# A dedicated pool for the loop's first-layer buffers, and a second level of Strassen's rule for one more product of the first MLP layer

## The chip, the cores and the metric

The kernel runs on one core of a Trainium2 chip, in one launch. The core has five engines with instruction streams of their own: PE (TensorE, matrix products; PEld is its loading of weights), DVE (VectorE), ACT (ScalarE), POOL (GpSimd) and SP (SyncE, which here only issues DMAs). [...] The metric is the device time of one execution in microseconds (us), median of several runs.

## The reference

Layer 0 is a deformable attention block with an MLP behind it, layer 1 a full self-attention block, on x of 2 x 512 x 32 x 32, all in float32. The change touches the end of the position-bias loop and the MLP of layer 0:

```python
bias = jnp.sign(pos) * jnp.log1p(jnp.abs(pos))
bias = jax.nn.relu(bias @ cpb_w1 + cpb_b1)          # 2 -> 128
bias = jax.nn.relu(bias @ cpb_w2 + cpb_b2)          # 128 -> 128
bias = (bias @ cpb_w3 + cpb_b3).reshape(b, GROUPS, H * W, Hd * Wd)
...
out = jnp.einsum('bchw,oc->bohw', out, out_w) + out_b[None, :, None, None]
x = x + out
xn2 = _bn(x, bn2_g, bn2_b)
h1 = jax.nn.gelu(jnp.einsum('bchw,oc->bohw', xn2, mlp_w1) + mlp_b1[None, :, None, None], approximate=False)
return x + jnp.einsum('bchw,oc->bohw', h1, mlp_w2) + mlp_b2[None, :, None, None]
```

`mlp_w1` is 2048 x 512 and `mlp_w2` is 512 x 2048. Layer 1 follows, and is not touched.

## The kernel before

**Order of the work.** From about 38 to 1881 us a loop of 256 steps runs the bias MLP: `st_layer1` builds h1 (128 x 4096) on DVE, `st_layer2` multiplies it on PE, ACT and DVE evict, and DMAs that add fold the results (`u`, `uo`, `uc`, `ub`). After that come the output projection (`project`), the MLP of layer 0 in eight units, and the attention of layer 1. Instructions are traced by a framework that allocates tiles in pools, inserts the semaphores, and settles at compile time the order on each engine; `tc.issue_after` pins one instruction behind another on its engine.

**Pools.** All buffers of the loop lie in one pool, `lp`: three h1 buffers of 16 KB a partition, and those named rx, u8, uo, uc, u4, ub, fb, ta, tb. When `lp` has been closed, the pools `xq` (`xs`, the residual x of 32 KB a partition, and `tx`) and `wp` (weights) are opened over the same addresses. The sixteen loads of `xs` (L1012, queue SP) are the first to use them; `project` reads `xs`.

**The eight units.** A unit is (b, p): image b, and quarter p of the 2048 hidden channels. Units 0 to 3 are image 0, units 4 to 7 image 1. Each has two halves:

- `layer1`: hidden = w1 quarter (512 x 512) times xb (512 x 1024). One level of the Strassen-Winograd rule turns it into seven products of 256 x 256 by 256 x 512. `PARTS[q]` names the sums of weights and of data that product q needs. Six of the seven (1 and 6, 4 and 7, 5 and 3, three sets) are split a second time by `twice`: seven steps, each one matmul per product of 128 x 128 by 128 x 256. The seventh, product 2, is plain: four matmuls of 128 x 128 by 128 x 512 (`second`, at time 21 among the steps; in unit 0 `first` at the start and `merge` at 21). In the trace every matmul stands as two instructions.
- `layer2`: w2 quarter times hidden, seven products of 256 x 256 by 256 x 512 by `multiply`, in the order 2, 1, 3, 5, 6, 7, 4.

`twice` puts the steps of the three sets in one order on PE by their times: set g has its products 1, 2, 6, 5, 7, 4, 3 at 7g + 0, 1, 3, 4, 6, 9, 12; fills such as the plain product have times of their own. So the tail of a unit on PE is: step 3 of set 1 (19), step 7 of set 2 (20), the plain product (21), step 4 of set 2 (23), step 3 of set 2 (26), and then layer 2. A step's sum grows in one PSUM bank: step 6 adds onto what ACT has just copied out of step 1, step 7 onto step 6, step 4 onto step 7, each after ACT's copy (L166, L170, L172, L176). DVE adds the rest (`plus`, L137): in `done(1)` c22, then c21, and ACT's `gelu(2)` (two instructions at L1096) makes the operand `hm[:, 2]` of layer 2's first product.

**PSUM.** Four tiles of two banks each are handed out in turn (`Turns`).

**Second-level sums.** `xe` holds the sums for the data (once for an image, on DVE: `sums`, `part`), `w1e` those for the weights: `load_inner` copies three blocks by SP DMAs (L996) and adds onto them by a chain of POOL DMAs (`gather`, L979). There is one `w1e` buffer, so the next unit's copies start when the last step has read it. Both leave out position 0, the operand of the plain product. Behind that chain POOL issues the adds for the unit after (w1x, w1t), and then folds w2t with four adds of its own (L119).

**Around images.** In unit 3 `normalise(1)` and the sums for image 1 are made, in unit 4 `finish(0)`, in unit 6 `blocks(0)` for layer 1, all beside the products.

Of the kernel before, what the change touches and what calls it, by code (L numbers as in the profile page):

```python
# [8 lines left out]
F32 = mybir.dt.float32  # L9
AF = mybir.ActivationFunctionType  # L10
ALU = mybir.AluOpType
# [3 lines left out]
P = 128  # L15
# [42 lines left out]
def conv_seq_kernel(ctx: ExitStack, tc: tile.TileContext, x, xt, kst, pst, cst, vec, wsm, outw, w1, w2, wl, wlt, brow, out):  # L58
# [62 lines left out]
    def spread(x, which=range(4)):  # L121
        for i in which:
            if i % 2 == 0:
                o, u = ((4, 0), (1, 3))[i // 2]
                nc.vector.tensor_tensor(x[o], x[u], x[1], ALU.subtract)  # L125
# [10 lines left out]
    def plus(out, a, b_, op=ALU.add):  # L136
        nc.vector.tensor_tensor(out, a, b_, op)  # L137
# [43 lines left out]
    FIRST_W, FIRST_X = (1, 0, 2, 3, 4, 5, 6), (1, 4, 0, 6, 5, 2, 3)  # L181
    AT_W, AT_X = ((0, 0), (1, 0), (1, 1), (0, 1)), ((0, 0), (0, 1), (1, 0), (1, 1))

    def inner_w(w, we, at=slice(1, 7), e=slice(0, 6)):
        return [w[:, at, k, P * n : P * n + P] for k, n in AT_W] + [we[:, e, j, :] for j in range(3)]

    def inner_x(x, xe, at=slice(1, 7), e=slice(0, 6)):
        return [x[:, at, k, 256 * n : 256 * n + 256] for k, n in AT_X] + [xe[:, e, j, :] for j in range(3)]


    def op_blocks(b, parts, wsum):
# [12 lines left out]
    groups = [(b, k, f) for b in range(B) for k in range(NCH) for f in range(2)]  # L204
    php = tc.tile_pool(name="ph", bufs=1, side="right")
    ph = php.__enter__()
    with tc.tile_pool(name="lp", bufs=2) as lp:


        def wake(src, *sizes):  # L210
# [10 lines left out]
        nc.scalar.activation(ones, ones, AF.Identity)  # L221

        for n in range(2):
            idle = lp.tile([P, 4 * HW], F32, tag="h1", name="idle", bufs=3)
# [352 lines left out]

        wls = [lp.tile([P, 2, NCH, C], F32, tag="h1", name="wl_s", bufs=3) for _ in range(2)]  # L580
# [8 lines left out]
        gs = lp.tile([P, 2, NCH, C], F32, tag="h1", name="gs", bufs=3)  # L589

        def weights(i):
            ps = [flat("psg") for _ in range(2)]
# [77 lines left out]
        def st_layer1(s):  # L670
            ta, tb = tabs[4 * s // KT]
            j = 4 * s % KT
            h1 = lp.tile([P, H, 4, W], F32, name="h1", bufs=3)
            a = ta[:, j : j + 4, :].rearrange("p t x -> p (t x)")
            b = tb[:, j // 4].rearrange("p y t -> p (y t)")
            step = H // 2 if s == 0 else H
            for y in range(0, H, step):
                nc.vector._custom_dve(  # L678
                    TENSOR_ADD_SAT,
                    out=h1[:, y : y + step].rearrange("p y t x -> p (y t x)"),  # L680
                    in0=a.unsqueeze(1).to_broadcast([P, step, 4 * W]),
                    in1=b[:, 4 * y : 4 * (y + step)].unsqueeze(2).to_broadcast([P, 4 * step, W]),
                    s0=FMAX, s1=0.0,
                )
            h1s[s] = h1
# [286 lines left out]
    with ExitStack() as top, tc.tile_pool(name="wp", bufs=1) as wp:  # L972
# [17 lines left out]
        def load_inner(i):  # L990
            if i >= len(units):
                return
            we = wp.tile([P, 6, 3, P], F32, name="w1e")
            w = inner_w(wts[units[i]][0], we)
            for o, u in ((4, 3), (5, 0), (6, 1)):
                nc.sync.dma_start(out=w[o], in_=w[u])  # L996
            copied.append(newest(mybir.EngineType.SP))
            gather(w)
            wts[units[i]].append(we)
# [81 lines left out]
            return go  # L1081

        def sums(xb):
            xe = mp.tile([P, 6, 3, 256], F32, tag="xe", name="xe")

            def part(g):
                spread([xb[:, j] for j in FIRST_X], ((0, 1, 3), (2,), ())[g])
                spread(inner_x(xb, xe, slice(2 * g + 1, 2 * g + 3), slice(2 * g, 2 * g + 2)))

            part(0)  # L1090
            return xe, part

        def layer1(p, we, w, xb, xe, hm, others=(), early=False):
            def gelu(blk, src, scale=1.0):
                for m in range(2):
                    nc.scalar.activation(  # L1096
                        hm[:, blk, m, :], src[:, m, :], AF.Gelu,
                        bias=col("mb1", 4 * p + 2 * (blk // 2) + m), scale=scale,
                    )

            c11, c12, c21, c22, r5, r3 = (hm[:, j] for j in range(6))

            def weights(q, j):
                a = FIRST_W[PARTS[q][0]]
                return [inner_w(w, we, a, a - 1)[j]]

            def moving(q, j):
                b_ = FIRST_X[PARTS[q][1]]
                return [inner_x(xb, xe, b_, b_ - 1)[j]]

            def dest(g, m, h):
                return hm[:, 2 * g : 2 * g + 2, m, 256 * h : 256 * h + 256]

            def done(g):
                if g == 0:
                    plus(c12, c12, c11)
                elif g == 1:
                    plus(c22, c22, c12)
                    plus(c21, c21, c22)
                    gelu(2, c21, -1.0)  # L1120
                else:
                    plus(c22, c22, r5)
                    gelu(3, c22, -1.0)
                    plus(c12, c12, r5)
                    plus(c12, c12, r3)
                    gelu(1, c12)

            def second():
                ps = mq.tile([P, 2, 512], F32, tag="ps2", name="sw")
                product(w, xb)(ps, 0, 0)  # L1130
                plus(c11, c11, ps)
                gelu(0, c11)

            def first():
                ps = mq.tile([P, 2, 512], F32, tag="ps2", name="sw")
                product(w, xb)(ps, 0, 0)
                nc.scalar.copy(hm[:, 6], ps)

            def merge():
                plus(c11, c11, hm[:, 6])  # L1140
                gelu(0, c11)

            plain = ((-1, first), (21, merge)) if early else ((21, second),)
            twice(mq, ((1, 6), (4, 7), (5, 3)), weights, moving, dest, done, (*plain, *others))
            spread([hm[:, j] for j in range(7)])

        def layer2(b, p, w, hm):
# [51 lines left out]
        for i, (b, p) in enumerate(units):  # L1199

            j, k = divmod(i, NCH)
            if k == 0:
                br = cp.tile([P, C], F32, tag="kz", name="br")
                nc.sync.dma_start(out=br, in_=brow[j].partition_broadcast(P))
            wr = f_pool.tile([P, C], F32, tag="ss", name="wr")
            nc.sync.dma_start(out=wr, in_=wlt[:, i])
            with tc.issue_after(copied[-1]) if i else nullcontext():
                load_first(i + 1)
            wa, we, wb = wts.pop((b, p))
            hm = cp.tile([P, 7, 2, 512], F32, tag="big", name="hm")  # L1210
# [388 lines left out]
```

## Time and profile before

| what | us |
|---|---|
| three runs | 2612.25, 2611.08, 2612.11; median 2612.11 |
| the profiled execution: time, and its span | 2612.84, 2610.9 |
| PE busy (share of span) | 2597.0 (99%) |
| DVE, ACT, POOL busy | 2299.8 (88%), 1754.3 (67%), 1002.0 (38%) |
| granted PE clock | 0.999 |
| matmul of 128 x 512 in `layer2` and the plain product (L1077): 448 and 64 instructions | 194.0 and 28.8 busy |
| units 1, 2, 5, 7, start to next start | 45.85, 45.85, 45.90, 45.90 |
| units 3, 4, 6 | 46.35, 46.20, 46.60 |

Busy PE time counts overlapping ends, so a matmul's listed mean (0.592 us for 512 columns) is longer than the distance between two of them (0.429 us). The distances are what adds up. The 1.9 us between span and time lie outside the first and last instruction.

### The profile page before, as it was taken

To read this page: it belongs to the slowest core of one execution; us is meant where nothing else is said; L and a number is where in the kernel's file an instruction comes from. 1 tells how busy PE (TensorE), PEld (TensorE's weight loads), DVE (VectorE), ACT (ScalarE), POOL (GpSimd) and SP (SyncE) were. 2 spreads that over 40 slices of the span, in tenths; PEclk is the share of its full clock that TensorE was granted. 3 is DMA by queue.
4 is the path that set the end of the run, shared out by engine and by line. 5 is a ranking of instruction groups with operands and counts; after the bars stand their busy time and mean duration, and the time that the engine had idled before them with its cause. 6 is when DMAs were issued, how large, how long until landed. Compare 5 with 4: busy or idle time off the path is not lost.

```text
span 2610.9 us, 49091 instructions
## 1 busy us (share of the span) xinstructions
PE 2597.0 (99%) x19644; PEld 1010.0 (39%) x19644; DVE 2299.8 (88%) x1459; ACT 1754.3 (67%) x2362; POOL 1002.0 (38%) x1154
## 2 busy tenths in 40 slices
PE   9999999999999999999999999999999999999999
PEld 3332333333233233323333333333355655646656
DVE  6999999999999999999999999999776586666656
ACT  5887888888888888888788777777633242314041
POOL 1344444444444444444454445444432333200100
PEclk9999999999999999999999999999999999999999
DMA  5889999899998999899999899999787768400202
GB/s 187 173 191 194 198 195 196 193 189 191 199 190 190 187 203 203 175 192 203 190 197 189 183 193 201 191 191 194 160 201 169 149 149 170 87 16 1 73 0 57
DMA packets 179172, 431.43 MB, mean 165 GB/s; under 512 B 30817, under 2 KB 79089, under 8 KB 176257
## 3 DMA queue, kind: packets, MB, share of 16 engines
q0 software_dynamic: 108416, 275.19, 59.0%
q1 hardware_dynamic: 70096, 152.80, 17.8%
q8 instruction: 155, 2.54, 0.4%
q14 instruction: 73, 0.59, 0.1%
q10 hardware_dynamic: 432, 0.31, 0.0%
HBM read 82.16 MB, written 6.55 MB: 34 GB/s over the span
## 4 chain that ended last, share of the span: by engine, by line
PE 76%; issue 7%; DVE 6%; DMA 6%; POOL 3%; ACT 1%; DVEq 0%; SPq 0%; POOLq 0%; ACTq 0%
PE ps L695 48%; PE sw L1077 7%; PE sw L1248 7%; PE sw L160 7%; DMA u<-uc 3%; POOL u L734 2%; PE sw L1346 2%; PE sw L1024 2%; DVE h L678 1%; DVE ub L715 1%; PE psg L597 1%; DMA uc<-uc 1%; DMA u<-u 1%; DVE hm L137 1%; PE sim L825 1%
## 5 line engine op out<-in xcount | busy, mean ns | idle before, releaser
L695 PE MATMUL ps<-h,cw 128*32 128x512 f32 x16384 | 1772.6, 593 | 2.8 <-ACT rx L705 1.4
L678 DVE CUSTOM_DVE_ANT_1 h<-ta,tb 128x4096 f32<-128x4096 f32 (+1 forms) x257 | 1130.8, 4400 | 27.1 <-PE ps L695 23.1
L695 PEld LDWEIGHTS ps<-h,cw 128*32 128x32 f32 x16384 | 528.1, 110 | 1216.0 <-issue 1156.5
L705 ACT ACTIVATE rx<-ps,sc 128x1024 f32<-128x1024 f32 x512 | 567.8, 1109 | 134.9 <-PE ps L695 113.4
L734 POOL DMA_DIRECT2D u<-u x429 | 434.6, 1498 | 3.6 <-issue 2.6
L707 ACT ACTIVATE ub<-ps,sc 128x1024 f32<-128x1024 f32 x256 | 308.0, 1203 | 91.5 <-PE ps L695 90.7
L715 DVE SCALAR_TENSOR_TENSOR ub<-rx,sc,ub 128x1024 f32<-128x1024 f32 x256 | 326.7, 1276 | 5.6 <-ACT ub L707 5.6
L717 POOL DMA_DIRECT2D uo<-ub x127 | 112.1, 882 | 566.2 <-DVE ub L715 543.3
L1077 PE MATMUL sw<-hm,w2t 128*128 128x512 f32 x448 | 194.0, 592 | 0.2 <-DVE hm L125 0.2
L707 ACT ACTIVATE uo<-ps,sc 128x1024 f32<-128x1024 f32 x128 | 154.0, 1203 | 43.8 <-PE ps L695 41.4
L715 DVE SCALAR_TENSOR_TENSOR uo<-rx,sc,uo 128x1024 f32<-128x1024 f32 x128 | 163.4, 1277 | 6.0 <-ACT uo L707 5.5
L734 POOL DMA_DIRECT2D u<-uc x126 | 126.0, 1282 | 21.6 <-DMA u<-uc 20.6
L717 POOL DMA_DIRECT2D u<-ub x64 | 55.8, 872 | 182.0 <-DVE ub L715 181.8
L1077 PEld LDWEIGHTS sw<-hm,w2t 128*128 128x128 f32 x448 | 85.1, 190 | 103.9 <-issue 97.9
L717 POOL DMA_DIRECT2D uc<-ub x64 | 55.0, 860 | 182.6 <-DVE ub L715 146.1
L137 DVE TENSOR_TENSOR hm<-hm,sw 128x512 f32<-128x512 f32 x79 | 57.7, 732 | 73.5 <-PE sw L160 51.5
L1412 POOL DMA_DIRECT2D xs<-rs x6 | 7.2, 1200 | 258.7 <-DVE rs L137 258.7
L734 POOL DMA_DIRECT2D uc<-uc x63 | 105.2, 1671 | 3.1 <-DMA uc<-ub 3.1
L734 POOL DMA_DIRECT2D uc<-uo x63 | 97.9, 1554 | 19.7 <-DMA uc<-uo 19.3
L707 ACT ACTIVATE uc<-ps,sc 128x1024 f32<-128x1024 f32 x64 | 76.9, 1202 | 25.3 <-PE ps L695 21.5
L658 ACT ACTIVATE ta<-fb,vs 128x512 f32<-128x512 f32 (+1 forms) x65 | 89.1, 1374 | 6.3 <-DMA fb<-fdr 6.3
L707 ACT ACTIVATE u<-ps,sc 128x1024 f32<-128x1024 f32 x64 | 77.0, 1203 | 24.2 <-PE ps L695 21.0
(297 smaller groups left out, 2635.1 us busy)
## 6 DMA issues: line engine op xcount, KB each, us to landing
uo<-ub POOLq DMA_DIRECT2D x127, 512.0 KB, 5.5
fb<-fdr SPq DMA_DIRECT2D x64, 512.0 KB, 6.1
u<-ub POOLq DMA_DIRECT2D x64, 512.0 KB, 6.6
uc<-ub POOLq DMA_DIRECT2D x64, 512.0 KB, 6.1
u<-u POOLq DMA_DIRECT2D x63, 256.0 KB, 7.0
u<-uo SPq DMA_DIRECT2D x63, 256.0 KB, 5.8
u<-uo POOLq DMA_DIRECT2D x63, 256.0 KB, 7.5
uc<-uc POOLq DMA_DIRECT2D x63, 256.0 KB, 8.4
```

Source lines behind the costliest of these rows:

```text
L137: nc.vector.tensor_tensor(out, a, b_, op)
L160: nc.tensor.matmul(bank[:, e, :], w, x, start=(q in (1, 2, 5) and e == k == 0), stop=True, skip_group_check=True,)
L658: nc.scalar.activation(ta.rearrange("p j x -> p x j")[:, :, j0:j1], fb[:, 0, :, j0:j1], AF.Identity, bias=col("cb1"), scale=col("w1x"),)
L678: nc.vector._custom_dve(TENSOR_ADD_SAT, out=h1[:, y : y + step].rearrange("p y t x -> p (y t x)"), in0=a.unsqueeze(1).to_broadcast([P, ste ...
L695: nc.tensor.matmul(ps[32 * q : 32 * q + 32, h, :], cw2[:, 32 * z : 32 * z + 32], h1[:, 16 * h : 16 * h + 16, q, :], start=True, stop=True,)
L705: nc.scalar.activation(o, ps, AF.Relu, bias=sc[:, 4 + z : 5 + z])
L707: nc.scalar.activation(o, ps, AF.Relu, bias=sc[:, 4 + z : 5 + z], scale=sc[:, z : z + 1])
L715: nc.vector.scalar_tensor_tensor(r[1], r[0], sc[:, z : z + 1], r[1], ALU.mult, ALU.add)
L717: nc.gpsimd.dma_start(out=sums[s][1], in_=sums[s][3], accum_op=ALU.add)
L734: nc.gpsimd.dma_start(out=out, in_=in_, accum_op=ALU.add)
L1077: nc.tensor.matmul(ps[:, m, :], w[:, a, k, m * P : (m + 1) * P], x[:, b_, k, :], start=(k == 0), stop=(k == 1),)
L1248: nc.tensor.matmul(ps[:, m, :], w[:, a, k, c + m * P : c + (m + 1) * P], x[b_][:, k, :], start=(k == 0), stop=(k == nk - 1),)
```

## The change

Three things.

1. The h1 buffers, and the tiles that share them (`idle`, `wl_s`, `gs`), move from `lp` to a pool `hp` of their own, opened before `lp`.
2. In the units with p > 0 (six of eight) product 2 is split by a second level too. Its seven steps, one matmul of 128 x 128 by 128 x 256 each, are fills at the times 19.5, 20.2, 20.4, 20.6, 24 and 27 (two). `gelu(2)` moves to the fill at 24, ahead of step 7. The additions that end c11 (`merge`) and c12 (`ends`) come at 27, behind step 3 of set 2. Layer 2 of these units takes its products in the order 2, 3, 1.
3. `xe` and `w1e` get position 0 (seven entries instead of six). `xe`'s is made by `part(3)` behind layer 2 of p = 0; `w1e`'s by the same DMAs, one sixth larger, except for p = 0.

```diff
-    def inner_w(w, we, at=slice(1, 7), e=slice(0, 6)):
+    def inner_w(w, we, at=slice(0, 7)):
...
-    with tc.tile_pool(name="lp", bufs=2) as lp:
+    with tc.tile_pool(name="hp", bufs=3) as hp, tc.tile_pool(name="lp", bufs=2) as lp:
...
-            h1 = lp.tile([P, H, 4, W], F32, name="h1", bufs=3)
+            h1 = hp.tile([P, H, 4, W], F32, name="h1")
...
-            we = wp.tile([P, 6, 3, P], F32, name="w1e")
-            w = inner_w(wts[units[i]][0], we)
+            we = wp.tile([P, 7, 3, P], F32, name="w1e")
+            w = inner_w(wts[units[i]][0], we, slice(i % NU == 0, 7))
...
-            xe = mp.tile([P, 6, 3, 256], F32, tag="xe", name="xe")
+            xe = mp.tile([P, 7, 3, 256], F32, tag="xe", name="xe")
             def part(g):
-                spread([xb[:, j] for j in FIRST_X], ((0, 1, 3), (2,), ())[g])
-                spread(inner_x(xb, xe, slice(2 * g + 1, 2 * g + 3), slice(2 * g, 2 * g + 2)))
+                spread([xb[:, j] for j in FIRST_X], ((0, 1, 3), (2,), (), ())[g])
+                spread(inner_x(xb, xe, slice(2 * g + 1, 2 * g + 3) if g < 3 else slice(0, 1)))
...
+        INNER = ((19.5, 1), (20.2, 2), (20.4, 6), (20.6, 5))
...
                 elif g == 1:
                     plus(c22, c22, c12)
                     plus(c21, c21, c22)
-                    gelu(2, c21, -1.0)
+                    if not split:
+                        gelu(2, c21, -1.0)
                 else:
                     plus(c22, c22, r5)
                     gelu(3, c22, -1.0)
-                    plus(c12, c12, r5)
-                    plus(c12, c12, r3)
-                    gelu(1, c12)
+                    if not split:
+                        ends()
+
+            def ends():
+                plus(c12, c12, r5)
+                plus(c12, c12, r3)
+                gelu(1, c12)
...
+            bank = {}
+            def inner(q):
+                a, x = PARTS[q]
+                if q in (1, 2):
+                    bank[q] = mq.tile([P, 2, 512], F32, tag="ps2", name="sw")
+                ps = bank[2][:, int(q in (3, 5)), 0:256] if q in (2, 3, 5) else bank[1][:, 0, 0:256]
+                nc.tensor.matmul(
+                    ps, inner_w(w, we, 0)[a], inner_x(xb, xe, 0)[x], start=q in (1, 2, 5), stop=True,
+                    skip_group_check=True,
+                )
+                m, h = {1: (0, 0), 6: (0, 1), 7: (1, 1), 4: (1, 0)}.get(q, (1, 1))
+                n = slice(256 * h, 256 * h + 256)
+                if q in (1, 6, 7, 4):
+                    nc.scalar.activation(hm[:, 6, m, n], ps, AF.Copy, scale=1.0 if m == 0 else -1.0)
+                elif q == 5:
+                    plus(c11[:, m, n], c11[:, m, n], ps, ALU.subtract)
+            def seventh():
+                gelu(2, c21, -1.0)
+                inner(7)
+            def close():
+                inner(3)
+                inner(4)
+                top = c11[:, 0, :].rearrange("p (h n) -> p h n", h=2)
+                plus(top, top, bank[2][:, :, 0:256])
+                merge()
+                ends()
-            plain = ((-1, first), (21, merge)) if early else ((21, second),)
+            if split:
+                plain = (*((t, lambda q=q: inner(q)) for t, q in INNER), (24, seventh), (27, close))
+            else:
+                plain = ((-1, first), (21, merge)) if early else ((21, second),)
...
-            multiply(mq, (2, 1, 3, 5, 6, 7, 4), product(w, hm), {
+            multiply(mq, (*first, 5, 6, 7, 4), product(w, hm), {
...
-            layer1(p, we, wa, xb, xe, hm, ((4, lambda: part(1)), (10, lambda: part(2))) if p == 0 else (), i == 0)
+            layer1(p, we, wa, xb, xe, hm, ((4, lambda: part(1)), (10, lambda: part(2))) if p == 0 else (), i == 0, p > 0)
...
-            layer2(b, p, wb, hm)
+            layer2(b, p, wb, hm, (2, 3, 1) if p else (2, 1, 3))
+            if p == 0:
+                part(3)
```

More of the change, by code (lines that the diff above doesn't have):

```diff
@@ L182, in conv_seq_kernel, with inner_x @@
     AT_W, AT_X = ((0, 0), (1, 0), (1, 1), (0, 1)), ((0, 0), (0, 1), (1, 0), (1, 1))
-    def inner_w(w, we, at=slice(1, 7), e=slice(0, 6)):
-        return [w[:, at, k, P * n : P * n + P] for k, n in AT_W] + [we[:, e, j, :] for j in range(3)]
-    def inner_x(x, xe, at=slice(1, 7), e=slice(0, 6)):
-        return [x[:, at, k, 256 * n : 256 * n + 256] for k, n in AT_X] + [xe[:, e, j, :] for j in range(3)]
+    def inner_w(w, we, at=slice(0, 7)):
+        return [w[:, at, k, P * n : P * n + P] for k, n in AT_W] + [we[:, at, j, :] for j in range(3)]
+    def inner_x(x, xe, at):
+        return [x[:, at, k, 256 * n : 256 * n + 256] for k, n in AT_X] + [xe[:, at, j, :] for j in range(3)]
     def op_blocks(b, parts, wsum):
@@ L223, in conv_seq_kernel @@
         for n in range(2):
-            idle = lp.tile([P, 4 * HW], F32, tag="h1", name="idle", bufs=3)
+            idle = hp.tile([P, 4 * HW], F32, tag="h1", name="idle")
             nc.gpsimd.memset(idle[:, 0:512], 0.0)
@@ L574, in later @@
                 yield from sample(ci)
-        wls = [lp.tile([P, 2, NCH, C], F32, tag="h1", name="wl_s", bufs=3) for _ in range(2)]
+        wls = [hp.tile([P, 2, NCH, C], F32, tag="h1", name="wl_s") for _ in range(2)]
         for o in range(NCH):
@@ L588, in conv_seq_kernel @@
             nc.sync.dma_start(out=ow_s, in_=outw)
-        gs = lp.tile([P, 2, NCH, C], F32, tag="h1", name="gs", bufs=3)
+        gs = hp.tile([P, 2, NCH, C], F32, tag="h1", name="gs")
         def weights(i):
@@ L1083, in sums, with layer1 @@
         def sums(xb):
-            xe = mp.tile([P, 6, 3, 256], F32, tag="xe", name="xe")
+            xe = mp.tile([P, 7, 3, 256], F32, tag="xe", name="xe")
             def part(g):
-                spread([xb[:, j] for j in FIRST_X], ((0, 1, 3), (2,), ())[g])
-                spread(inner_x(xb, xe, slice(2 * g + 1, 2 * g + 3), slice(2 * g, 2 * g + 2)))
+                spread([xb[:, j] for j in FIRST_X], ((0, 1, 3), (2,), (), ())[g])
+                spread(inner_x(xb, xe, slice(2 * g + 1, 2 * g + 3) if g < 3 else slice(0, 1)))
             part(0)
             return xe, part
-        def layer1(p, we, w, xb, xe, hm, others=(), early=False):
+        INNER = ((19.5, 1), (20.2, 2), (20.4, 6), (20.6, 5))
+        def layer1(p, we, w, xb, xe, hm, others=(), early=False, split=True):
             def gelu(blk, src, scale=1.0):
@@ L1104, in weights @@
                 a = FIRST_W[PARTS[q][0]]
-                return [inner_w(w, we, a, a - 1)[j]]
+                return [inner_w(w, we, a)[j]]
             def moving(q, j):
                 b_ = FIRST_X[PARTS[q][1]]
-                return [inner_x(xb, xe, b_, b_ - 1)[j]]
+                return [inner_x(xb, xe, b_)[j]]
             def dest(g, m, h):
@@ L1141, in merge, with layer2 @@
                 gelu(0, c11)
-            plain = ((-1, first), (21, merge)) if early else ((21, second),)
+            bank = {}
[28 more added lines that the diff above has]
+                plain = ((-1, first), (21, merge)) if early else ((21, second),)
             twice(mq, ((1, 6), (4, 7), (5, 3)), weights, moving, dest, done, (*plain, *others))
             spread([hm[:, j] for j in range(7)])
-        def layer2(b, p, w, hm):
+        def layer2(b, p, w, hm, first):
             def own(j):
```

## The prediction

> **What bounds the kernel.** I read the page first, then the busy time by stretches (one stretch a unit), PE's waits between 1860 and 2330 us, the chain of waits there, and the timelines of the unit tails.
>
> ```profile
> span 2610.9 us, 49091 instructions
> ...
> 1985.15:2031.00 45.85, 45.85 (x149) 27.96 (x149) 28.01 (x29) 12.32 (x20) 13.69 (x13) 1.00 0.71 150
> ...
> 2076.85:2123.20 46.35, 46.07 (x149) 27.83 (x149) 36.36 (x39) 19.93 (x30) 15.42 (x13) 1.00 0.73 156
> ...
> 2215.30:2261.90 46.60, 46.31 (x149) 27.75 (x148) 32.95 (x33) 12.32 (x20) 13.38 (x10) 1.00 0.64 113
> ```
>
> Columns of a stretch: length, then busy time of PE, PEld, DVE, ACT, POOL, then PE's clock. In unit 1 PE has no gap: 45.85 of 45.85. Units 3 and 6 are longer by 0.50 and 0.75. Every edit in the units is therefore paid or earned in PE's time, if the other engines keep up.
>
> ```profile
> PE sw L1024 <- DMA xs<-in_x: 1.2, 1, 1.2
> PE sw L160 <- DVE hm L137: 0.4, 2, 0.3
> PE sw L1077 <- DVE hm L125: 0.2, 1, 0.2
> ```
>
> PE's only other waits: 1.2 us in `project` put down to a load of xs, and 0.6 us behind DVE in units 3, 4 and 6.
>
> **The split product.** The chain of waits has the tail of unit 1:
>
> ```profile
> 2001.80 3.43 PE sw L1077 x8
> 2005.24 1.73 PE sw L160 x8
> 2006.96 24.03 PE sw L1077 x56
> ```
>
> Removed: 8 instructions of 512 columns, 3.43 us. Added: 7 matmuls of 256 columns, 14 instructions at 1.73 / 8 = 0.216, so 3.03 us. Gain 0.40 a unit, 6 x 0.40 = 2.4 us. That is all the work PE loses.
>
> **Does the tail keep up?** Before, the 3.43 us in one piece hid whatever DVE and ACT had to finish; now PE returns to the same bank after short steps.
>
> ```profile
> 2001.84 0.60 ACT L172 ACTIVATE hm<-sw 128x512 f32<-128x512 f32 x1 [2.00 <-PE sw L160]
> 2004.76 1.33 ACT L1096 ACTIVATE hm<-hm,vs 128x512 f32<-128x512 f32 x2 [2.33 <-DVE hm L137]
> 2006.14 0.60 ACT L176 ACTIVATE hm<-sw 128x512 f32<-128x512 f32 x1
> ```
>
> Let s = 2000.78, where step 7 of set 2 starts. In new PE time (0.43 an inner step, 0.86 a pair): inner 1 to s+0.43, step 7 to 1.29, inner 2, 6, 5 to 2.59, step 4 to 3.45, inner 7 to 3.88, step 3 to 4.75, inner 3 to 5.18, inner 4 to 5.61, then layer 2 (before: 6.02). ACT sees a result 0.2 after PE's issue (2001.64 to 2001.84). Its copies of inner 1 and 6 fall into idle time. From s+3.65 it has step 4's copy (0.60), inner 7's copy and both halves of `gelu(2)` (1.33; input c21 from DVE at s+3.95, as before). Copies of 128x256 are not in the trace from PSUM; 64x256 takes 0.36 (L554), 128x512 takes 0.59; I use 0.40. If inner 7's copy goes first, it ends at 4.65, inner 4 isn't late, and gelu ends at 5.35 and 6.0; layer 2's first matmuls need the first half at 5.61 and the second 0.86 later. No stall. If both halves go first, they end at 5.6, the copy at 6.03, and inner 4 starts at 6.07 instead of 5.18: 0.89 lost. The program has gelu ahead of the copy in the text, but the order is settled at compile time by what is ready: before, step 4's copy stood later in the text than `gelu(0)` and ran first. I take the first order, and keep the second as a rival.
>
> **DVE and the order of layer 2.** New on DVE: 128x256 for inner 5 (0.41, the row of L443), 128x512 for the top (0.69), and the merge over 128x1024 (1.22) in place of the plain product's addition of the same size: +1.1 a unit, 1.9 of it behind step 3 of set 2 while PE gives only the two inner steps, 0.86, of extra time. In the clean units that is hidden. After step 3, DVE has its addition (0.69), c22 (1.22), top (0.69) and merge (1.22): the merge ends 4.1 after step 3, its gelu (1.33) 5.5, and PE wants it as third product 0.86 + 2 x 3.43 = 7.7 after. Two additions for c12 (2.4), their gelu (1.33) and x4 (1.22) follow: 9.1, wanted by the fourth product at 11.2. The cover is gone in unit 3, where DVE runs without a gap from 2099.25 to 2129.8 and PE already waits on it: up to 1.9 - 0.86 = 1.0, at least 0; I take 1.0. In unit 6 `blocks(0)` sits in the same place (PE waited 0.24 for x4): 0 to 1.0, I take 0.5. `part(3)` adds four 128x256 operations, 1.65 us twice, into gaps of DVE of 10.9 us (before 1985.18) and 2.6 us (before 2169.45): nothing; without that cover 1.65.
>
> **The chain for w1e.** Same DMAs, 448 KB instead of 384. Tightest is unit 2's:
>
> ```profile
> 2010.71 1.46 POOL L979 DMA_DIRECT2D w1e<-w1x  x1 [8.83 <-PE sw L1077]
> 2011.58 2.06 POOL L979 DMA_DIRECT2D w1x<-w1x  x1
> 2023.43 1.43 POOL L979 DMA_DIRECT2D w1e<-w1e  x1 [9.79 <-DMA w1e<-w1x]
> 2029.04 1.43 POOL L979 DMA_DIRECT2D w1e<-w1e  x1 [4.18 <-DMA w1e<-w1e]
> ```
>
> The addition at 2023.43 lands 5.6 later, 2029.0; PE first reads that block at 2031.0 + 1.73 = 2032.7: 3.7 spare. Growth of 64 KB: SP copy 0.35 (3.9 against 3.2 for 256 KB), the first addition, 12 us beside the 1.8 MB load, at most a sixth, 1.9, the second 0.35 (5.6 against 4.9), POOL's issue 0.29 twice (1.43 against 0.85): 3.2 in all. Hidden, by half a microsecond. Behind it POOL's queue holds the additions for the unit after and then the w2t fold, which comes 1 to 3 us later. Layer 2 needs the fold's last block late enough (in unit 2 the fold ended at 2048.5, the second product would start at 2056), so PE doesn't wait for it; but the fold runs beside DVE:
>
> ```profile
> 2087.43 2.52 DVE L137 TENSOR_TENSOR hm<-hm 128x1024 f32<-128x1024 f32 x1
> ```
>
> This is an addition of two SBUF tiles that takes 1.22 elsewhere, started 0.16 after a fold (2087.27); others beside folds took 1.48 to 2.29. Moved later, the folds of units 1, 2, 3 and 6 meet c22 and c21. Each may cost 0.25 to 1.3; c21 can be 0.95 late before gelu's first half is. I take nothing and keep up to 1 us for each of four units.
>
> [...]
>
> **The pool.** SP's waits:
>
> ```profile
> SPq L1012 <- DMA uc<-ub: 9.5, 1, 9.5
> ...
> SPq L1012 <- PE sim L825: 4.3, 1, 4.3
> ```
>
> The xs loads waited for buffers of the loop that don't lie under them, until 1888.09. xq needs 32 KB for xs and 14 for tx, hp has 3 x 16, so they need only the last read of h1, at 1881.0: 7 us earlier. PE's 1.2 us (to 1895.87) doesn't all go: DVE's additions that free the bank ended at 1895.66, held by ACT's copy at 1894.22, which waits for no load. Gain 0.2; bounds 0 and 1.2.
>
> **Sum.** -2.4 - 0.2 + 1.0 + 0.5 = -1.1: the profiled execution from 2612.84 to 2611.7. It stood 0.7 above the median, so in terms of the median 2612.1 - 1.1 = 2611.0. The loop (1850 us) and layer 1 (300 us) keep their times.
>
> **Rivals.**
> - ACT takes gelu first. For: the text, and both ready within 0.15 us. A clean unit then goes from 6.02 to 6.5, +0.48; units 2 and 5, where c21 came 0.7 later (gelu at 2189.76 in unit 5, ending 6.0 after its s), +0.9: 4 x 0.48 + 2 x 0.9 = 3.7. The waits in units 3 and 6 vanish behind it, so 2612.1 + 3.7 - 0.2 = 2615.6; with the folds on top, 4 x 1, 2619.6. It ends slower as soon as inner 4 waits over 0.40 a unit, beyond 0.2% with a third of the fold cost.
> - Everything hidden, waits too: -2.4 - 1.2 and the 0.6 us behind DVE gone: 2607.9. Against: DVE's gapless stretch.
> - The w1e chain late: 1 us in five units, 2611.0 + 5 = 2616. For: 0.5 us of spare. Against: the other units' chains land 3 to 6 us sooner.
> - The pool does nothing because the loads wait for all of lp still: 2611.2, inside the forecast.
>
> **Numbers.** Forecast 44% (its own range 2609.5 to 2612.5), gelu first 35%, all hidden 13%, late chain 8%. Range 2608.0 to 2618.0. A measurement of this kernel tells about 0.2%, 5.2 us, from no change: faster means under 2606.9, the far end of the all-hidden case, 4%; slower over 2617.3, half of the gelu case (18%) and a third of the late chain (2%): 20%; the rest, 76%, within.
>
> **What would show it.** Right: units 1 and 7 at 45.45, PE without gaps between step 4 and layer 2; inner 7's copy ahead of `gelu(2)` on ACT; xs loads at 1881. Wrong: PE waiting for an ACT copy (hm) just ahead of layer 2; DVE additions of two SBUF tiles over 2 us at the tail; PE waiting for a w1e DMA in a unit's third step; unit 3 or 6 unchanged or shorter.

## The result, and the profile after

| | before | after |
|---|---|---|
| median of 22 executions each | 2612.12 us | 2615.28 us |
| lowest to highest | 2611.08 to 2618.53 | 2613.48 to 2629.99 |
| ratio after to before, 95% interval | | 1.002 [1.0012, 1.0028] |
| the profiled execution, its span | 2612.84, 2610.9 | 2628.86, 2627.1 |

The change made the kernel slower by about 3 us. That is inside the range of the prediction and on the wrong side of its forecast, 2611.0. The profiled execution of after is one of the longest of its 22, so its parts have to be kept apart: what every execution has, and what only some have.

The stretches of units 1, 3, 4, 5 and 6 of after (columns: length, then busy time of PE, PEld, DVE, ACT and POOL, PE's clock, DMA share, GB/s):

```profile
1999.15:2044.93 45.78, 45.72 (x156) 28.82 (x154) 29.31 (x31) 13.78 (x24) 18.84 (x15) 1.00 0.79 162
2091.12:2136.97 45.85, 45.73 (x156) 28.73 (x155) 35.71 (x39) 21.17 (x34) 15.09 (x13) 1.00 0.79 163
2136.97:2184.55 47.58, 46.25 (x150) 27.87 (x148) 39.11 (x46) 18.47 (x26) 15.95 (x13) 1.00 0.73 152
2184.55:2231.96 47.41, 45.95 (x155) 28.73 (x154) 32.19 (x31) 13.88 (x24) 24.76 (x17) 1.00 0.83 177
2231.96:2278.26 46.30, 45.72 (x155) 28.82 (x154) 34.02 (x35) 13.77 (x24) 15.92 (x12) 1.00 0.78 131
```

Only unit 7 came to the 45.44 us that the split allows (45.85 before). Units 4 and 5 grew by 1.4 and 1.6. The eight units together take 371.42 us, 1.96 more than before (369.46), where the prediction had 0.9 less.

PE's waits from 1850 to 2370 us of after (waited for: us in total, times, longest):

```profile
PE sim L825 <- issue: 7.3, 1, 7.3
PE sim L825 <- DMA uc<-ub: 4.6, 1, 4.6
PE sw L1157 <- DVE hm L137: 1.3, 3, 0.6
PE sw L1024 <- ACT sx L868: 1.2, 1, 1.2
PE sw L1077 <- DVE hm L125: 1.1, 1, 1.1
PE sw L1077 <- DVE xs L137: 0.9, 1, 0.9
```

The two longest are new and lie at the end of the loop, ahead of `project`. The third, fifth and sixth are in the units, and DVE ends all of them. The 1.2 us in `project` are still there, now put down to ACT.

The span grew by 16.2 us. Unit 0 starts at 1952.28 instead of 1938.13: 14.15 at the end of the loop. The units add 1.96, the rest 0.1. The first part differs from execution to execution: the shortest executions of after are 2.4 us above the shortest of before (2613.48 and 2611.08), little more than the units' share, and 8 of the 22 lie over 4 us above that.

**The end of the loop.** The chain of waits of after, from 1871 to 1899 us (start, length, what):

```profile
1879.22 1.21 ACT ub L707
1880.43 0.03 issue
1880.46 1.30 DVE ub L715
1881.76 0.63 issue
1882.39 13.06 DMA uc<-ub
1895.45 0.14 issue
1895.59 3.63 PE sim L825 x14
```

The loop's last addition, a DMA of 512 KB that adds `ub` onto `uc`, was in flight for 13.06 us. On SP's queue of after the loads stand beside it (start, length, line, what):

```profile
1879.21 3.92 SPq L1012 DMA_DIRECT2D xs<-in_x  x8
1883.17 0.77 SPq L986 DMA_DIRECT2D w1x<-in_w  x1
1883.99 12.96 SPq L1012 DMA_DIRECT2D xs<-in_x  x8
```

With a pool of their own for h1, the loads of xs start at 1879.21 instead of 1888.09, as the change has it. The stretches of after show what that meets (last column GB/s, the column of 0.66 and 0.67 is PE's clock):

```profile
1880.00:1890.00 10.00, 3.57 (x10) 1.04 (x12) 1.28 (x1) 0.43 (x1) 1.67 (x2) 0.66 0.96 258
1890.00:1900.00 10.00, 5.38 (x24) 1.54 (x20) 0.00 (x0) 0.00 (x0) 0.00 (x0) 0.67 1.02 391
```

The DMA engines are full while the last additions run, and PE stands. But the loop's chain of additions was late in this execution before any load began. The same addition of POOL onto `uc`, in before and then in after (in brackets the wait ahead of it):

```profile
1868.09 0.84 POOL L734 DMA_DIRECT2D uc<-uo  x1 [2.03 <-DMA uc<-uo]
1873.13 0.84 POOL L734 DMA_DIRECT2D uc<-uo  x1 [8.31 <-DMA uc<-uo]
```

So two things come together, a late chain and early loads.

**The tails of the units.** Unit 5 of after: POOL's folds, DVE's additions at the same time, and PE behind them (start, length, what; in brackets the idle time before, and what ended it):

```profile
2200.36 7.26 POOL L119 TENSOR_TENSOR w2t<-w2t 128x512 f32<-128x512 f32 x4
2207.57 8.96 POOL L119 TENSOR_TENSOR gg<-gg 128x512 f32<-128x512 f32 x4
```
```profile
2201.33 1.70 DVE L137 TENSOR_TENSOR hm<-hm 128x1024 f32<-128x1024 f32 x1
2203.56 1.69 DVE L137 TENSOR_TENSOR hm<-hm 128x1024 f32<-128x1024 f32 x1
2206.98 6.13 DVE L137 TENSOR_TENSOR hm<-hm 128x1024 f32<-128x1024 f32 x3
```
```profile
2205.64 0.70 PE L1157 MATMUL sw<-xb,w1e 128*128 128x256 f32 x2 [0.38 <-DVE hm L137]
2218.15 6.25 PE L1077 MATMUL sw<-hm,w2t 128*128 128x512 f32 x14 [1.07 <-DVE hm L125]
```

The additions of two SBUF tiles take 1.69 to 2.29 us instead of 1.22 from set 1's c22 to the first addition of `ends`: 0.48 + 0.47 and 6.13 - 3.49 = 2.64, 3.6 us of DVE's time in one tail. (Three such additions back to back without a fold take 3.49.) PE feels 0.38 of it at inner 3, which goes back to the bank that DVE must have read for inner 5, and 1.07 where layer 2 wants the sums that DVE makes next.

Unit 4 has a wait of another kind. PE and DVE of after:

```profile
2181.01 3.70 PE L1077 MATMUL sw<-hm,w2t 128*128 128x512 f32 x8 [0.89 <-DVE xs L137]
```
```profile
2179.13 0.68 DVE L1258 SCALAR_TENSOR_TENSOR wr<-wr,br 128x512 f32<-128x512 f32 x1
2179.74 1.22 DVE L137 TENSOR_TENSOR xs<-xs,sw 128x1024 f32<-128x1024 f32 x1
```

The last product of layer 2 waits for a PSUM slot that DVE has yet to empty; the addition that empties it (product 3's) stands behind the eight of `finish(0)`.

### The profile page after: what moved, and what is told of

It is laid out like the page before. It is cut to its first block, busy times and chain, and to the rows that moved or that the text cites. A ratio compares the mean times of both kernels' runs of the same rounds, so it can differ in the third digit from the quotient of the medians.

```text
span 2627.1 us, 49212 instructions
## 1 busy us (share of the span) xinstructions
PE 2599.4 (99%) x19680; PEld 1016.0 (39%) x19680; DVE 2310.1 (88%) x1479; ACT 1764.0 (67%) x2386; POOL 1015.3 (39%) x1154
## 4 chain that ended last, share of the span: by engine, by line
PE 91%; DVE 4%; issue 2%; DMA 2%; ACT 1%; POOL 1%; DVEq 0%; ACTq 0%; POOLq 0%; SPq 0%
PE ps L695 64%; PE sw L1290 7%; PE sw L160 6%; PE sw L1077 6%; PE sw L1388 2%; PE sw L1024 2%; DVE hm L137 1%; PE psg L597 1%; PE sim L825 1%; DMA uc<-uc 1%; PE psx L1366 1%; DVE xs L137 0%; DMA uc<-ub 0%; POOL u L734 0%; PE sw L1157 0%
## 5 line engine op out<-in xcount | busy, mean ns | idle before, releaser
L137 DVE TENSOR_TENSOR hm<-hm,sw 128x512 f32<-128x512 f32 (+2 forms) x85 | 56.7, 672 | 68.3 <-PE sw L160 48.8
```

## The experiments

Each experiment was timed against before on its own chip, mostly with eleven executions. The unit lengths are from start to next start on PE, in us, to 0.01 (the prediction read them to 0.05):

| kernel | units 0 to 7 | sum |
|---|---|---|
| before | 46.85 45.85 45.85 46.40 46.16 45.85 46.65 45.85 | 369.46 |
| after | 46.87 45.78 46.19 45.85 47.58 47.41 46.30 45.44 | 371.42 |
| e1, pool alone | 46.85 45.85 46.27 46.17 47.09 45.85 46.33 45.85 | 370.26 |
| e2, split alone | 46.85 45.84 45.90 45.89 48.15 48.03 45.80 45.44 | 371.90 |
| e3, after and a gate | 46.85 46.54 45.92 45.62 48.68 47.78 45.93 45.44 | 372.76 |
| e4, split, folds on DVE | 48.65 47.14 51.36 54.04 48.70 53.81 51.48 46.07 | 401.25 |
| e5, split, pinned folds | 46.83 45.44 45.43 45.44 47.45 45.44 45.44 45.98 | 367.45 |
| e6, split, turns reset | 46.86 46.08 45.63 46.17 46.43 46.92 46.37 45.44 | 369.90 |
| e7, e5 and e6 | 46.83 45.44 45.44 45.43 46.29 45.44 45.44 46.68 | 366.99 |
| e8, e7, pool and gate | 46.83 45.44 45.44 45.44 46.29 45.44 45.44 46.57 | 366.89 |
| e9, before, pinned folds | 46.83 45.85 45.85 45.85 46.17 45.85 46.33 46.05 | 368.78 |
| e10, e8, gg earlier | 46.83 45.44 45.44 45.44 46.28 45.44 45.44 45.44 | 365.75 |
| e11, e8 without the gate | 46.83 45.44 45.44 45.44 46.28 45.96 45.44 46.44 | 367.27 |

Each row is one profiled execution, and where the folds on POOL start differs from one to the next. Unit 1, for example, is the same program in after, e2, e3 and e6 and took 45.78, 45.84, 46.54 and 46.08. With the folds on POOL, a sum is good to about 1 us.

### e1: the pool alone, on the kernel before

```diff
-    with tc.tile_pool(name="lp", bufs=2) as lp:
+    with tc.tile_pool(name="hp", bufs=3) as hp, tc.tile_pool(name="lp", bufs=2) as lp:
...
-            h1 = lp.tile([P, H, 4, W], F32, name="h1", bufs=3)
+            h1 = hp.tile([P, H, 4, W], F32, name="h1")
```

> The kernel before with the pool for h1 alone. Theory A (the xs and w1x loads, 6 MB, now start at about 1880 us beside the loop's last additions and hold them up, so that PE waits at the third layer's last matmuls): most executions 2612 to 2614, some 3 to 16 us above, a wide spread; in the profile the last addition uc<-ub takes well over the 4.5 us of before to land and PE waits at L825. Theory B (the spread and the loss come from the split product): 2611.9, as before, with the narrow spread of before, and PE's 1.2 us wait for xs gone.

Measured: 2612.46 us, ratio 1.001 [1.0, 1.002]. Eight of twelve executions lie between 2611.4 and 2612.6, where before lies; four lie between 2619.9 and 2622.0. The pool alone makes the long executions longer and leaves the short ones alone. The profiled execution is a short one: its last addition was issued at 1877.74, two microseconds ahead of the loads, and landed in 4.8 us (4.5 in before). Its unit 4 is 0.9 longer than before's, though nothing was changed there: an addition of two SBUF tiles took 2.90 us beside a fold, and PE waited 0.7 for it.

### e2: the split alone, h1 back in lp

```diff
...
-            h1 = hp.tile([P, H, 4, W], F32, name="h1")
+            h1 = lp.tile([P, H, 4, W], F32, name="h1", bufs=3)
```

> The changed kernel with h1 back in lp: the split product alone. Theory A: the spread of before, and 1 to 2 us above before (2613 to 2614), since the eight units took 1.9 us more in the changed kernel's profile. Theory B: the wide spread stays, 2613 to 2630, median near 2615. If the prediction's sum for the units had been right: 2611.2.

Measured: 2614.81, ratio 1.0013 [1.0004, 1.0021]. The units are as long as in after (371.90), so their loss belongs to the split. PE's waits have the same entries, without the one of 4.6 us for the last addition:

```profile
PE sim L825 <- issue: 3.6, 1, 3.6
PE sw L1024 <- DMA xs<-in_x: 1.2, 1, 1.2
PE sw L1077 <- DVE hm L125: 1.2, 1, 1.2
PE sw L1157 <- DVE hm L137: 1.2, 3, 0.8
PE sw L1077 <- DVE xs L137: 1.1, 1, 1.1
```

The chain of the loop is late in this execution too (3.6 us at L825), with no load near it. The pool is not what makes it late.

Neither expectation is met as a whole: four of the eleven executions lie between 2618.2 and 2621.1, a wider spread than theory A had, and none lies near the 2630 of theory B. The profiled execution is one of the four, and it gives the loads their price. POOL issued the addition onto `uc` at 1873.19 after a wait of 8.28 and the last one at 1882.44, both within 0.1 us of after. Here the last one landed in 4.5 us, and unit 0 starts at 1943.07; in after it took 13.06, and unit 0 starts at 1952.28. The same lateness costs 4.9 us without early loads and 14.2 with them.

### e3: after, with the loads of xs held until the last addition has landed

```diff
+        last = sums[NS - 2][1]
+        nc.sync.dma_start(out=dp.tile([P, 2], F32, name="gate"), in_=last[:, 0, 0:2])
+        gate = newest(mybir.EngineType.SP)
...
-                nc.sync.dma_start(out=xs[:, o, b, n], in_=xv[:, o, b, n])
+                with tc.issue_after(gate):
+                    nc.sync.dma_start(out=xs[:, o, b, n], in_=xv[:, o, b, n])
```

> The changed kernel, with one transfer of 1 KB that reads the result of the loop's last addition put ahead of the xs loads on SP's queue, so that the loads start after it. Theory A: the spread goes, 2613 to 2614, like the split alone. Theory B, or a pool that hurts by its place in memory: as the changed kernel, median about 2615 with runs to 2630.

Measured: 2613.99 (2611.49 to 2614.99), ratio 1.0001 [0.9993, 1.001]. No execution lies above 2615. SP and PE of e3:

```profile
1882.66 0.33 SPq L937 DMA_DIRECT2D gate<-uc  x1
1883.08 5.26 SPq L1016 DMA_DIRECT2D xs<-in_x  x8
```
```profile
1882.74 0.62 PE L825 MATMUL sim<-uc,w3u 128*32 128x512 f32 x2 [0.26 <-DMA uc<-ub]
```

The last addition was issued at 1878.09 and PE had it at 1882.74, 4.65 later instead of 13. The units stay long (372.76), so their loss has nothing to do with the gate. That no execution is long isn't the gate's doing alone: e2 holds the loads back as well and had four. What the gate takes away is what the loads add to a late chain; e8 and e11 are the clearer pair for it.

### e4: the split, with the folds on DVE and free to be placed

```diff
-            fold(nc.gpsimd, [w[:, j] for j in range(7)])
+            fold(nc.vector, [w[:, j] for j in range(7)])
```

and gg's fold in the same way.

> The split product alone (h1 in lp), with the folds of w2t and of gg, 4 additions of 128x512 for each, on DVE instead of POOL. If the units' loss comes from folds that meet DVE's additions of two SBUF tiles: DVE's additions at the unit tails fall back to 1.22 us, units 2, 3, 5 and 6 lose their extra, and the time is 2 to 3 us below the split alone, about 2610.5 to 2611. If the loss comes from the order of the banks or of ACT instead: within 0.7 us of the split alone. If DVE can't take the 2.7 us more a unit: above it.

Measured: 2647.46, ratio 1.013 [1.0117, 1.0143]. This experiment failed as a test. The compile-time order put the folds on DVE ahead of evictions, where they wait for the load of w2t, and PE waited 23.7 us in nine places for the evictions behind them. It says what a misplaced fold cost here, nothing on the meeting of folds and additions.

### e5: the split, with the w2t folds pinned late in layer 1 on DVE, and gg two units later

```diff
-            fold(nc.gpsimd, [w[:, j] for j in range(7)])
...
+            def folds():
+                with tc.issue_after(newest(mybir.EngineType.DVE)):
+                    fold(nc.vector, [wb[:, j] for j in range(7)])
+            others = ((4, lambda: part(1)), (10, lambda: part(2))) if p == 0 else ()
+            layer1(p, we, wa, xb, xe, hm, (*others, (16.5, folds)), i == 0, p > 0)
...
-            if i == NU:
+            if i == NU + 2:
```

> The split product alone (h1 in lp), the w2t folds on DVE again, but now pinned in its order ahead of step 3 of set 1 (time 16.5), where DVE was idle 2.7 us and w2t has landed, and the load and fold of gg moved from unit 4 to unit 6. Collision theory: no DVE addition of 128x1024 at a unit's tail over 1.3 us, PE's waits at L1157 gone, units 1, 2, 5, 7 at 45.45 us, the eight units 1.5 to 2.5 us shorter than in the split alone; fast executions near 2610.5 to 2611.5. If the unit tails are late for another reason (ACT's gelu ahead of inner 7's copy, the longer DVE queue): within 0.7 us of the split alone, waits at L1157 still there.

Measured: 2610.39 (2609.89 to 2616.37), ratio 0.9991 [0.9982, 1.0]. Units 1, 2, 3, 5 and 6 come to 45.43 or 45.44, the whole 0.41 of the split, although DVE has 2.6 us more to do in each; no addition of two SBUF tiles at a unit's tail takes over 1.3 us. The units are 4.5 us shorter than in e2, where 1.5 to 2.5 was expected. Unit 4 keeps its wait, and unit 7, which now has gg's fold, is 0.54 too long.

### e6: the split, with the PSUM turns reset in each unit

```diff
+        turns = mq.pools
         for i, (b, p) in enumerate(units):
+            mq.pools = turns
```

> The split product alone, with the turn of the PSUM pools set back to the same start in every unit (15 tiles a split unit had shifted it by one). Bank theory: unit 4's wait of 0.9 to 2.0 us for an addition to xs (last product of layer 2) goes, as in the kernel before, and nothing else changes: 1 us below the split alone, about 2612.5 to 2613 in fast executions. If that wait comes from DVE's longer queue: it stays, same time as the split alone.

Measured: 2613.74 (2610.54 to 2617.53), ratio 1.0005 [0.9996, 1.0014]. Unit 4 goes from 48.15 to 46.43 and the wait for `DVE xs` is gone, while the other units keep theirs. In e6 product 3's addition comes just as late, at 2171.12 behind `finish(0)`, but the last product starts ahead of it, at 2170.25: it has another slot.

Why it has one can be worked out from the program's text. The turn goes once to a pool of one slot and then three times to a pool of three. A split unit takes 15 tiles, a plain one 14, so 59 were taken ahead of unit 4 in after and 56, a multiple of four, in before. Counted on from there, product 3 and the last product both fall to the pool of one slot in after, and the last must wait; in before and in e6 both fall to the pool of three, where another slot was free. The traces don't name the slots, so this is argued, but it fits every run: after, e2, e3, e4 and e5 have the wait (0.9 to 2.0 us), and no kernel without the split or with the reset has it.

### e7 and e8: both, then with the pool and the gate as well

> Both edits, pinned folds on DVE and the turn of the banks, on the split product alone. If both theories hold: the eight units at 368 to 369 us, 0.5 to 2 us below the kernel before's 369.5, fast executions 2610 to 2611. If only one: the better of the two single runs.

> As the one before, and with h1 in its own pool and the xs loads behind the loop's last addition. If the pool has nothing to give once the loads are held back: as without the pool, 2610 to 2611 in fast executions, and late executions no worse than before's 2618. If early loads have something to give: up to 1.2 us less.

Measured: e7 2608.7 (2607.82 to 2609.79), ratio 0.9984 [0.9975, 0.9993]; e8 2608.24 (2607.75 to 2609.8), ratio 0.9981 [0.9972, 0.999]. Both beat both kernels, before by 4 us and after by over 6, and both are 1 to 2 us under the 2610 to 2611 expected. Three stretches of e8, units 1, 3 and 5:

```profile
1983.98:2029.42 45.44, 45.44 (x155) 29.06 (x154) 30.93 (x35) 13.64 (x24) 12.35 (x11) 1.00 0.78 164
2074.86:2120.30 45.44, 45.44 (x155) 29.05 (x154) 37.58 (x43) 21.02 (x34) 7.94 (x8) 1.00 0.77 159
2166.59:2212.03 45.44, 45.44 (x156) 29.05 (x155) 31.09 (x35) 13.65 (x24) 10.07 (x10) 1.00 0.80 164
```

PE has no gap. The pool and the gate together bring nothing that the intervals tell from none.

### e9: the kernel before with the pinned folds

> The kernel before with one thing changed: the w2t folds run on DVE, pinned late in the second set of the first layer, and the loop's table gg is loaded and folded two units later. No split, no pool. Theory (the folds on POOL cost only where they met DVE's additions, in the units at 46.2 to 46.7; the split's own gain is 0.41 a unit whatever the folds do): units 1, 2, 3, 5 and 6 at 45.85, the eight units 368.0 to 368.6 us against 369.46, time 0.9 to 1.4 us under before, near 2611.0; and the split with the same folds (2610.4, units 367.45) then stands under this kernel by what the split gives less unit 4's turn of the pools. Rival (most of what the pinned folds brought with the split was not the split's): units 1 to 6 at 45.4 to 45.6 already here, 366.5 to 367.5, near 2609.5. Second rival (3.8 us of folds on DVE in the tail need the split's slack): units over 46.2, 2613 or more.

Measured: 2610.79 (2609.89 to 2616.95), ratio 0.9994 [0.9985, 1.0003]; units 368.78, 0.2 over the range given, with unit 6 at 46.33 instead of the 45.85 expected. PE's waits from 1930 to 2330 us:

```profile
PE sw L1076 <- DVE hm L125: 0.2, 1, 0.2
PE sw L160 <- ACT hm L170: 0.2, 1, 0.2
PE sw L160 <- DVE hm L137: 0.2, 1, 0.2
```

Unit 3 is 45.85 without the split as well, so its 0.5 us in the kernel before were a fold's and not DVE's load. The moved folds are worth 0.7 us of the units by themselves; e7 stands another 1.8 lower, which is the split's with its turns reset.

### e10: e8 with gg's load ahead of the next w2t load

```diff
+            if i == NU + 2:
+                with tc.issue_after(newest(mybir.EngineType.SP)):
+                    gg = f_pool.tile([P, 7, 2, 256], F32, tag="vp", name="gg")
+                    load_g(gg, 0)
             load_second(i + 1)
```

> The best kernel so far (split, phase, pinned folds, pool and gate; 2608.2) with gg's load issued ahead of the next unit's w2t load, so that its fold on POOL (6.0 us, from 2266.4, 9 us into unit 7) comes some 10 us or more earlier and no longer meets the additions ahead of the pinned folds. Theory (unit 7's 46.57 against 45.44 is that meeting: the addition of 1.88 us beside the fold, PE's wait of 0.87 behind it): unit 7 at 45.4 to 45.7, the others unchanged, 2607.2 or a little under. Rival (the pinned folds alone make DVE late in unit 7, or the moved fold meets other additions): unit 7 at 46.3 or more, or unit 6 longer by as much, time unchanged within 0.4 us.

Measured: unit 7 is 45.44, as expected. POOL of e10 has gg's fold in unit 6, beside layer 2, and DVE's addition 10.7 us into unit 7, just ahead of the pinned folds, takes 1.22 again (1.88 in e8):

```profile
2247.84 4.20 POOL L119 TENSOR_TENSOR gg<-gg 128x512 f32<-128x512 f32 x2
2254.45 3.18 POOL L119 TENSOR_TENSOR gg<-gg 128x512 f32<-128x512 f32 x2
```
```profile
2267.34 1.22 DVE L137 TENSOR_TENSOR hm<-hm 128x1024 f32<-128x1024 f32 x1
```

The eight units take 365.75. The median is 2608.13 (2607.09 to 2612.08), ratio 0.9982 [0.9973, 0.9991]. The profile shows the 1.1 us; the times, taken on another chip than e8's, can't tell them, so the expectation holds for the unit and is open for the time.

### e11: e8 without the gate

> The best kernel so far with the gate taken out: the pool stays, so the xs loads are free to start at about 1881 again, beside the loop's last additions. Theory (early loads cost only where the loop's chain of additions is late already, and then 3 to 16 us): most executions at 2607.7 to 2609.8, as with the gate, but 2 to 5 of 11 above 2614, which neither the kernel with the gate nor the one with neither pool nor gate showed; in a late profile PE waits over 4 us at line 825. Rival (the late executions belonged to the order of the folds, or to nothing in these kernels): none above 2611. Second rival (the loads cost in every execution): the fastest ones 1 us or more above 2608.2.

Measured: 2610.76 (2607.88 to 2618.5), ratio 0.9997 [0.9986, 1.0007]. The shortest executions are as short as e8's, four of eleven lie between 2613.8 and 2618.5, and no execution of e8 lies above 2609.8. Five lie in the range expected for most. The early loads cost only some executions, up to 10 us. The profiled execution was not one of these (PE waited 0.4 us for the last addition), so the wait of over 4 us was not seen here, only in after.

## Why the prediction went wrong

**What the split gives** was right. A unit loses 0.41 us where the working had 0.40, once nothing else is in the way (e5, e7, e8, e10).

**"I take nothing and keep up to 1 us for each of four units"** is the step that failed in the units. The folds were seen, their shift of 1 to 3 us was about right (0.3 to 4.0 in units 1, 2, 3, 5 and 6; unit 1's began 14.1 us into the unit instead of 11.4), and so was what they meet. The price wasn't nothing. Against 45.44, units 1, 2, 3 and 6 of after lost 0.34, 0.75, 0.41 and 0.86, and unit 5, which the step left out, 1.97. There POOL has gg's fold right behind w2t's, and three more additions of two SBUF tiles after c22 and c21 met folds as well. The three waits at line 1157, 0.34, 0.38 and 0.58 us in units 2, 5 and 6, are all ahead of inner 3, and in units 1 and 3 the same step starts 0.2 and 0.3 us late.

The prediction measured the slack at the wrong place. Its 0.95 us is what c21 may be late before `gelu(2)` is. But inner 3 writes the bank that DVE reads for inner 5, in an addition that stands right behind c21, and there less than half a microsecond is spare: in unit 1 of e8 that addition ends at 2004.05 and inner 3 starts at 2004.53. In the kernel before, PE had 3.43 us of plain product at this place. Unit 2 of before shows that it was cover enough: its c22 met a fold and took 0.7 us too long, and the unit kept its 45.85.

```profile
2047.62 1.94 DVE L137 TENSOR_TENSOR hm<-hm 128x1024 f32<-128x1024 f32 x1
```

What a meeting costs can be read from the rows. One is the addition of 1.48 us in unit 5 of before:

```profile
2186.03 1.48 DVE L137 TENSOR_TENSOR hm<-hm 128x1024 f32<-128x1024 f32 x1
```

When this addition began, the fold instruction on POOL had 0.40 us left (to 2186.43), and the addition ended at 2187.52, 1.08 after it. So do the others: in the units of before and after, 19 additions of 128x1024 began with 0.1 to 1.4 us of a fold instruction left, and each ended 1.08 to 1.11 us after the end of that instruction, whatever was left of it. An addition alone takes 1.22, so by these times each stood until the fold instruction was all but done (0.1 us). A meeting cost the rest of the fold instruction that ran, less 0.1 to 0.15: 0.26 us for the 0.40 here, 1.30 for the 1.43 ahead of the row of 2.52, 0.5 to 1.1 each in unit 5 of after. The range that the prediction gave for a meeting, 0.25 to 1.3, was about right, and what it kept back, up to 1 us for each of four units, was nearer than the nothing that it took: they lost 2.4 and gained 4 x 0.41 = 1.6.

**Units 3 and 6: "+1.0" and "+0.5"** were wrong in mechanism. DVE's stretch without a gap in unit 3 was taken for the limit. With the folds elsewhere both units go to 45.44, though DVE does the fold's work too. In unit 3 the wait of the kernel before was a fold beside an addition: e9 has 45.85 there without any split, and the row of 2.52 us that the prediction shows was its trace. In unit 6 e9 still has 46.33, so of its 0.8 us in the kernel before only about 0.3 was a fold's; with the split and the folds elsewhere it is gone, and why no run tells. The prediction charged 1.5 us to DVE's load and nothing to the meetings, and it was the other way round.

**Unit 4** was in no step. The fifteenth PSUM tile of the split units moves the turn of the slots, and in the unit where `finish(0)` holds DVE it put the last product on a slot that came free late: 0.9 us in after, 1.1 in e2.

**The pool: "Gain 0.2; bounds 0 and 1.2".** The gain was as small as said: the wait of 1.2 us only changed its releaser. The bounds were wrong, since they had no loss. The step followed the loads to their own end and didn't ask what they run beside: 4 MB of xs and 1.8 MB of w1x, freed 8.9 us earlier, run beside the additions that PE waits for next. Before, the loads stood behind those additions because they shared a pool. The false wait was a gate. Its worth is seen only where the chain is late: 9.2 us between the late executions of e2 and after, 0.3 in the landing of the timely one of e1.

**The rivals.** ACT did take `gelu(2)` ahead of inner 7's copy, and it cost nothing. ACT and PE of after in unit 7:

```profile
2298.20 1.32 ACT L1098 ACTIVATE hm<-hm,vs 128x512 f32<-128x512 f32 x2
2299.43 0.37 ACT L1164 ACTIVATE hm<-sw 128x256 f32<-128x256 f32 x1
```
```profile
2298.80 0.59 PE L1157 MATMUL sw<-xb,w1e 128*128 128x256 f32 x2
2299.24 1.02 PE L1077 MATMUL sw<-hm,w2t 128*128 128x512 f32 x2
2300.09 0.59 PE L1157 MATMUL sw<-xe,w1t 128*128 128x256 f32 x2
```

PE's order too is settled at compile time: the first two instructions of layer 2 stand ahead of inner 4, so PE uses the gelu while ACT copies. The copy of 128x256 took 0.36 to 0.39 (0.40 estimated). The rival's price of 3.7 us had PE in the order of the program's text. The late chain of w1e stayed hidden; its half microsecond of spare shows once, as a wait of 0.3 us in unit 5 of e11. The time of "all hidden" (2607.9) was reached by e8, but with three edits more.

**The balance.** The split takes 6 x 0.41 = 2.5 us off the units. Units 1, 2, 3, 5 and 6 stand 4.3 above 45.44 and unit 4 stands 1.3 above e7's; units 3 and 6 of before had 1.35 of that already. With 0.15 left over, in units 0 and 4, that is the 1.96 measured: -2.46 + 4.33 + 1.29 - 1.35 + 0.15. The median lost 3.2 us; the rest, 1.2 us, is put down to the long executions, without a run that shows it for the median. With the gate (e3) the loss against before, on another chip, is 1.5.

What makes the loop's chain of additions late in some executions stays open. The profiles of e2, e4 and e6, which have no early load, show it, and the order on DVE, ACT and POOL in the loop is the same in all kernels; the long executions of before, up to 2618.5, were not profiled. The lateness goes with one pair of transfers: SP's copy of `uo` to `uc` (256 KB, the one at 1866.57 in after) landed in 2.3 to 2.6 us where it was issued at most 0.25 us behind POOL's addition of `ub` onto `u` (512 KB), in 4.3 where it came 0.4 us behind it (e9), and in 5.8 to 6.3 where it came 2.2 to 3.2 us behind it (after, e2, e4 and e6). No run moved the one or the other, so this isn't shown to be the cause.

## What to carry to other kernels

When an operation moves by a few microseconds, list what it will run beside, not only what waits for it: here the same folds cost nothing or 2 us by their place. Before you free a transfer from a wait, look at what it was held behind; if that is on the path, leave the wait or put a gate in its place (here a pool with a gate brought no more than no pool, e8 and e7). Look for slack at every reader of a bank, not only at the next one on the path. Where buffers are handed out in turn, count what one pass takes: a count that isn't a multiple of the slots changes which slot comes late.

## What the runs showed of the hardware

- An addition of two SBUF tiles on DVE (128x1024) and a fold instruction on POOL took turns here: the one that started second ended about 1.1 us after the first one's end. In the units of before and after this was 1.08 to 1.11 for the additions (19 of 19 that began with 0.1 us or more of the fold left) and 1.13 to 1.15 for the folds (16 of 18), where they take 1.22 and 1.27 alone. So 1.22 us became 1.37 to 2.29 on DVE in the units of after, and gg's fold instructions had a median of 2.25 us there against 1.27 in e7.
- PE's clock in after fell to 0.50 in the wait of 7.27 us, 4.1 us after the end of the matmul ahead of it (at 1883.2), stood at 1.00 from 1890.1, and fell to 0.50 again in the wait of 4.62 us, 2.5 us after the matmul ahead of that one (at 1893.5); from 1900.4 it was 1.00. Between 1886 and 1890, at 0.50, four matmul instructions of 512 columns took 1.68 us from start to next start instead of 0.86 (e3). So these waits cost more than their length: from the first matmul on `uc` to the first on `ub` PE took 5.54 us (1895.59 to 1901.13), and 3.30 in e3 (1882.74 to 1886.04). In e2, with a wait of 3.6 us, the clock was 0.66 between 1880 and 1890.
- An adding DMA of 512 KB landed in 4.5 us where the loads were held back (before, e2, e3), in 4.8 where it was issued 2 us ahead of them (e1), and in 13.06 where it was issued 3 us behind the first of 5.8 MB of them (after).
